# Quarter sums of the adjacency made by adding DRAM transfers, and layer 2 of the last two pairs run apart, in a four-layer graph network

## The chip, the cores and the metric

The kernel runs on one core of one Trainium2 chip. The metric is the device time of one execution in microseconds (us), given as the median of several runs. One further execution was profiled; the traces and the page below are of that one.

## What is computed

Inputs are `x` (8 batches, 2048 nodes, 64 channels, float32) and one 2048 x 2048 matrix `adj`. Four layers follow each other, each with a residual and a layer norm:

```
# layer 0: y0 = x, y1 = A x, y2 = 2 A y1 - x; node-wise weights from a 16-wide embedding
out = einsum('bnki,nkio->bno', x_g, w) + b
# layer 1: masked attention, att = softmax(where(adj > .5, leaky(s1_i + s2_j), -9e15))
h_prime = einsum('bij,bjc->bic', att, h);  elu
# layer 2: agg = einsum('ij,bjh->bih', adj + I, x W^T + b) / deg
# layer 3, three times: effects = A v;  v = relu([v, effects] W1^T + b1) W2^T + b2
x = layernorm(x + layer(x))        # after each layer
```

Almost all of the multiplying is the product of `A` (or `A + I`) with a 2048-row matrix: twice per batch in layer 0, once in layer 2, three times in layer 3, and the attention product of layer 1.

## The kernel before, in words

**Tiles.** Two batches of 64 channels make a pair; there are four pairs, and a pair's activations fill a 128-column matrix of 16 row tiles in SBUF (`SX[p]`, and the shared buffers `SA`, `SB`, `SH`). The transposed matrix stays in DRAM. It is read in tiles of 128 partitions x 2 x 512 float32, 512 KB each, 32 to a sweep (4 column chunks `c` by 8 row blocks `q`). A tile is loaded by the SP queue into a ring of six buffers (`a_ring`, `fetch`, `refill`), in the order of the list `order_of_a`. One sweep for one pair is 64 matmuls of 128 x 512 (line 1093), each in two float32 passes. Results of a chunk are accumulated in one of two PSUM banks (`acc_ring`).

**Order.** All engines' instruction orders are written at build time by a planner (class `Plan`): each thread (a Python generator) names the engine that it wants next and what it waits for, and the planner runs the one that can begin first, by ready time and then by rank. What comes out is one fixed order for each engine. The sweeps have the lowest rank (1000) and fill TensorE.

**Stages.** TensorE makes the layer-0 products first (`first_product`, `second_product`, and line 601 for the node-wise weights), then layer 2 and the three steps of layer 3 for pair 0 and then for pair 1, and meanwhile the attention products (line 836) of all pairs, for which VectorE works nearly without a pause: it finds row maxima over mask rows `mr` (line 731, `scores`), and adds and subtracts rows for the weights (lines 809 and 822, `weights`). Mask rows (`mr`, 512 KB) and mask columns (`mk`, 256 KB), and the broadcast rows `s2b`, `s1b` and `mb` (1 MB each) are loaded by the GpSimd (POOL) queue, which also stores.

**The last two pairs** are handled jointly, because one product of a 2048 x 2048 matrix with a 2048 x 256 matrix can be made in seven quarter products instead of eight. The quarters of `A` are a11, a12, a21, a22 (first index: output half, second: contracted half); those of the right side are B11, B21 (first pair `p`) and B12, B22 (second pair `o`).

- `joint_layer2` (line 1188) does layer 2 of both pairs at once: each tile of `A` is loaded once and used for both pairs (line 1212), four PSUM banks being open. The four tiles at the same place in the four quarters come one after the other, and thread `sums` (line 1159) makes from them on VectorE, in tiles of 128 x 1024 (line 1172), s1 = a21 + a22, s2 = s1 - a11, s3 = a11 - a21 and s4 = a12 - s2. Each is stored to DRAM by the POOL queue (line 1174). Where the tile in SBUF holds `A + I`, `pure` (line 1149) loads the plain tile once more.
- `joint_layer3` (line 1247) does the three steps with the seven products a11 B11, a12 B21, s2 T1, s3 T2, a22 T3, s1 T0, s4 B22 (line 1299). The T are differences of the B (`sums_of_u`). Parts of the result are put together on VectorE (`combine`), and the v-term of the layer is added by a seed matmul (line 1284, and line 1347 for one quarter).

After a product's chunk come short chains over several engines. After layer 2: copy out of PSUM (`z_evict`), product with W (line 981), residual and norm on VectorE and ScalarE, transposes (line 1015), product for `u` (line 1028). After a step of layer 3: relu (`h_evict`), then line 1028, or line 1048 and the final norm and store (`last_chunk`, `store`).

Priority of the scores: `layer1` starts `scores(p)` with rank `10 + p`, and its loads of `s2b` wait in the planner until all mask rows are stored (`"rows"`).

Of the kernel before, what the change touches and what calls it, by code (L numbers as in the profile page):

```python
# [17 lines left out]
P = 128  # L18
# [6 lines left out]
B = 8  # L25
# [118 lines left out]
def resnorm_d4_kernel(  # L144
# [182 lines left out]
    for e in range(2):  # L327
# [20 lines left out]
        for m in ("s1", "s2", "s3", "s4")  # L348
# [84 lines left out]
    def row_tile(t, an, k, done):  # L433
        yield "ACT", [done]
        dg = tiny([P, 1], "dg", 2)
        nc.scalar.activation(an, an, AF.Copy, accum_out=dg)
        done = plan.run("ACT", act(N) + 0.2, done)
        yield "DVE", [done, mr_ring]
        nc.vector.tensor_scalar_add(dg, dg, 1.0)
        nc.vector.reciprocal(rdeg[:, t : t + 1], dg)  # L440
        mk, km = mr_ring.take([P, N], "mr", BF16)
        nc.vector.tensor_scalar(mk, an, THRESHOLD, NEG_INF, ALU.is_le, ALU.mult)
        done = plan.run("DVE", 1.13 + 0.26, done)
        bc_ring.give(k, done)
        nc.gpsimd.dma_start(by_row[t], mk)
        done = plan.dma("DMA", 512, done)
        mr_ring.give(km, done)
        at["by_row", t] = done
        if all(("by_row", i) in at for i in range(NT)):
            at["rows"] = done  # L450
# [208 lines left out]
    def layer1(p):  # L659
# [38 lines left out]
        plan.start(10 + p, scores(p, sv, xc, s_rows, done))  # L698

    def scores(p, sv, xc, s_rows, done):  # L700
        s2b = []
        for e in range(2):
            yield "DMA", [bc_ring, done, "rows"]
# [228 lines left out]
    JOINT = (NPAIR - 2, NPAIR - 1)  # L932
# [9 lines left out]
    def z_evict(p, c, pa, give, done):  # L942
# [4 lines left out]
        give(done)  # L947
# [180 lines left out]

    RQ = AQ // 2

    def quarters(k, r):

        return [(k, r), (k, r + RQ), (k + 2, r), (k + 2, r + RQ)]

    def order_of_joint():
        for k in range(2):
            for r in range(RQ):
                order_of_a.extend((c, q, True) for c, q in quarters(k, r))
        for s in range(3):
            for m in ("a11", "a12", "s2", "s3", "a22", "s1", "s4"):  # L1140
                i, j = {"a11": (0, 0), "a12": (0, 1), "a22": (1, 1)}.get(m, (0, 0))
                for k in range(2):
                    for r in range(RQ):
                        if m[0] == "a":
                            order_of_a.append((k + 2 * i, r + RQ * j, False))
# [3 lines left out]
    def pure(k, r):  # L1149

        yield "SP", [("group", k, r), *([xg_ring] if len(xg_ring.freed) > 1 else [NEVER])]
        got = []
        for c, q in (quarters(k, r)[i] for i in (0, 3)):
            t, kt = xg_ring.take([P, 2, CW], "pure")
            nc.sync.dma_start(t, tile_of_adj(c, q))
            got.append((t, kt, plan.dma("SP", 512, xg_ring.t)))
        return got

    def sums(k, r, taken):

        tiles4 = [(t, kt, got) for t, kt, got, _ in taken]
        own = {}
        if r // 2 == k:
            own = dict(zip((0, 3), (yield from pure(k, r))))
        a11, a12, a21, a22 = ((own.get(i) or tiles4[i])[0] for i in range(4))
        ready = [(own.get(i) or tiles4[i])[2] for i in range(4)]

        def out_of(m, a, b, op, *after):
            yield "DVE", [bc_ring, *after]
            t, kt = bc_ring.take([P, 2, HALF], m)  # L1170
            t = t.rearrange("p a b -> p (a b)")[:, 0 : 2 * CW].rearrange("p (t n) -> p t n", n=CW)
            nc.vector.tensor_tensor(t, a, b, op)
            done = plan.run("DVE", dve(2 * CW), *after)
            nc.gpsimd.dma_start(sum_tiles[m][k, r], t)  # L1174
            bc_ring.give(kt, plan.dma("DMA", 512, done))
            return t, done

        s3, d3 = yield from out_of("s3", a11, a21, ALU.subtract, ready[0], ready[2])
        s1, d1 = yield from out_of("s1", a21, a22, ALU.add, ready[2], ready[3])
        s2, d2 = yield from out_of("s2", s1, a11, ALU.subtract, d1)  # L1180
        s4, d4 = yield from out_of("s4", a12, s2, ALU.subtract, d2)
        for (_, kt, _, free), d in zip(taken, (d2, d4, d1, d1)):
            a_ring.give(kt, max(free, d))
        for _, kt, _ in own.values():
            xg_ring.give(kt, d2)
        refill()

    def joint_layer2():
        p, o = JOINT
        at["group", 0, 0] = 0.0  # L1190
        for k in range(2):
            pas = {}
            for r in range(RQ):
                taken = []
                for i, (c, q) in enumerate(quarters(k, r)):
                    n = next(used)
                    if r == 0 and i in (0, 2):
                        if i == 0:
                            yield "PE", [po_ring, ("x2", p), ("x2", o)]
                            t2, kp = po_ring.take([P, 2, CW], "po")  # L1200
                            pas[c] = [(t2[:, e, :], kp) for e in range(2)]
                        else:
                            pas[c] = []
                            for e in range(2):
                                yield "PE", [acc_ring]
                                pas[c].append(acc_ring.take([P, CW], "acc"))
                    for e, pair in enumerate(JOINT):
                        yield "PE", [("a", n)]
                        t, kt = a_tiles[n]
                        for b in range(2):  # L1210
                            m = 2 * q + b
                            nc.tensor.matmul(
                                pas[c][e][0],
                                lhsT=SX[pair][:, m, :],
                                rhs=t[:, b, :],
                                start=(r == 0 and i in (0, 2) and b == 0),
                                stop=(r == RQ - 1 and i in (1, 3) and b == 1),
                            )
                        done = plan.run("PE", mm(CW, 2), ("a", n))
                        if r == RQ - 1 and i in (1, 3):  # L1220
                            if i == 3:
                                give = lambda t, kk=pas[c][e][1]: acc_ring.give(kk, t)
                            else:
                                give = give_half(pas[c][e][1])
                            plan.start(1, z_evict(pair, c, pas[c][e][0], give, done))
                    del a_tiles[n]
                    taken.append((t, kt, at["a", n], done))
                    if i == 0:
                        nxt = (k, r + 1) if r + 1 < RQ else (k + 1, 0)
                        at[("group", *nxt)] = plan.free["PE"]  # L1230
                    spent[0] += 1
                plan.start(5, sums(k, r, taken))
                refill()

    halves_left = {}

    def give_half(kp):
        def give(t):
            left, last = halves_left.pop(kp, (2, 0.0))
            if left == 1:  # L1240
                po_ring.give(kp, max(t, last))
            else:
                halves_left[kp] = (1, max(t, last))

        return give

    def joint_layer3():
        p, o = JOINT
        U, _ = e_ring.take([P, 2, HALF], "u23")
        T12, _ = e_ring.take([P, 2, HALF], "t12")  # L1250
        T34, _ = e_ring.take([P, 2, HALF], "t34")
        T = [
            t[:, i, :].rearrange("p (t n) -> p t n", n=P) for t in (T12, T34) for i in range(2)
        ]
        for s in range(3):
            up, uo = u_of(p, s), u_of(o, s)
            B11, B21, B12, B22 = up[:, 0:8], up[:, 8:16], uo[:, 0:8], uo[:, 8:16]
            plan.start(0, sums_of_u(s, T, B11, B21, B12, B22))
            u = lambda pair, half: lambda k: ("u", pair, s, 2 * half + k)
            t = lambda i: lambda k: ("t", s, i, k)  # L1260
            seed = gv if s else w31v
            held = {}

            for m, B, need, evict, seeded in (
                ("m1", B11, u(p, 0), None, None),
                ("m2", B21, u(p, 1), None, (p, 0)),
                ("m6", T[1], t(1), "u2", None),
                ("m7", T[2], t(2), "u3", None),
                ("m4", T[3], t(3), "c21", (p, 1)),
                ("m5", T[0], t(0), "c22", None),  # L1270
                ("m3", B22, u(o, 1), "c12", (o, 0)),
            ):
                for k in range(2):
                    if m == "m2":
                        pa, ka = held[k]
                        yield "PE", [("m1", s, k)]
                    else:
                        yield "PE", [acc_ring, need(0)]
                        pa, ka = acc_ring.take([P, CW], "acc")
                    go_on = m == "m2"  # L1280
# [197 lines left out]
```

## Time and profile before

| | us |
|---|---|
| median of 3 runs | 2132.62 (2131.99 to 2137.06) |
| the profiled execution | 2133.99 |
| its span in the trace | 2132.2 |
| TensorE busy / idle in the span | 2067.3 / 64.9 |
| VectorE busy | 1496.4 |
| joint layer 2 begins / joint layer 3 begins / last large matmul ends | 1652 / 1782 / 2121 |
| granted TensorE clock, mean | 0.994 |

How to read the profile: engines are PE (TensorE matmul), PEld (its weight loads), DVE (VectorE), ACT (ScalarE), POOL (GpSimd) and SP (SyncE). `L1093` is line 1093 of the kernel. In a table of windows each row gives the stretch, its length, then for each engine the busy time and (x...) its instructions, then the granted clock, the share of the 16 DMA engines' time that is busy, and GB/s. In a timeline, each row gives start, duration, engine, line, operation, output and inputs, and in brackets how long the engine was idle before it and what ended that. A float32 matmul is recorded as two passes, so 64 matmuls show as x128.

### The profile page before, as it was taken

To read this page: it belongs to the slowest core of one execution; us is meant where nothing else is said; L and a number is where in the kernel's file an instruction comes from. 1 tells how busy PE (TensorE), PEld (TensorE's weight loads), DVE (VectorE), ACT (ScalarE), POOL (GpSimd) and SP (SyncE) were. 2 spreads that over 40 slices of the span, in tenths; PEclk is the share of its full clock that TensorE was granted. 3 is DMA by queue.
4 is the path that set the end of the run, shared out by engine and by line. 5 is a ranking of instruction groups with operands and counts; after the bars stand their busy time and mean duration, and the time that the engine had idled before them with its cause. 6 is when DMAs were issued, how large, how long until landed. Compare 5 with 4: busy or idle time off the path is not lost. (4 is left out here: it accounts for less than half of the span.)

```text
span 2132.2 us, 19037 instructions
## 1 busy us (share of the span) xinstructions
PE 2067.3 (97%) x6325; PEld 914.9 (43%) x6325; DVE 1496.4 (70%) x1908; ACT 974.9 (46%) x1794; POOL 213.0 (10%) x374
## 2 busy tenths in 40 slices
PE   8999999999999999999798999989999999999998
PEld 3444444433433443433343453443444444444444
DVE  2226647998799999789998979999796455120214
ACT  0025424567776566777624857336575012000002
POOL 2310000100110100000010101011010110000000
PEclk9999999999999999999899999999999999999999
DMA  9799835634443465554388778897776777878785
GB/s 303 267 333 345 306 105 209 218 122 136 138 137 131 159 238 169 170 178 150 124 309 299 254 267 285 279 339 239 264 236 234 290 255 273 280 254 281 251 288 188
DMA packets 208740, 495.85 MB, mean 233 GB/s; under 512 B 20274, under 2 KB 28594, under 8 KB 204530
## 3 DMA queue, kind: packets, MB, share of 16 engines
q1 hardware_dynamic: 165058, 347.62, 48.0%
q0 software_dynamic: 39360, 144.92, 19.7%
q10 hardware_dynamic: 4224, 2.10, 0.4%
q8 instruction: 50, 0.82, 0.2%
q14 instruction: 48, 0.39, 0.1%
HBM read 446.14 MB, written 46.33 MB: 231 GB/s over the span
## 5 line engine op out<-in xcount | busy, mean ns | idle before, releaser
L1093 PE MATMUL acc<-a,SX 128*128 128x512 f32 x1024 | 465.8, 598 | 9.6 <-DMA SX<-in_x 6.6
L1093 PE MATMUL acc<-a,SA 128*128 128x512 f32 x768 | 348.6, 596 | 13.1 <-DMA a<-in_adj_t 12.4
L817 ACT ACTIVATE e<-e,sv 128x1024 f32<-128x1024 f32 x256 | 280.1, 1154 | 114.4 <-DVE e L809 110.6
L731 DVE CUSTOM_DVE_ANT_0 junk<-s2b,mr 128x2048 bf16<-128x2048 f32 x128 | 292.7, 2287 | 5.2 <-DMA mr<-by_row 3.9
L624 ACT ACTIVATE terms<-yp,emb_sb 128x128 f32<-128x128 f32 x896 | 243.5, 400 | 113.6 <-PE yp L601 113.3
L1093 PEld LDWEIGHTS acc<-a,SX 128*128 128x128 f32 x1024 | 190.3, 191 | 242.2 <-issue 229.6
L822 DVE TENSOR_TENSOR e<-e,mb 128x2048 f32<-128x2048 f32 x128 | 290.0, 2286 | 6.0 <-ACT e L817 5.4
L809 DVE TENSOR_TENSOR e<-s1b,mk 128x2048 f32<-128x2048 f32 x128 | 289.1, 2286 | 6.5 <-PE po L836 4.0
L825 ACT ACTIVATE e<-e 128x2048 f32<-128x2048 f32 x128 | 245.0, 1928 | 67.5 <-DVE e L822 67.2
L601 PE MATMUL yp<-SH,xgT 128*128 128x512 f32 x512 | 246.9, 607 | 3.3 <-ACT sv L358 3.3
L836 PE MATMUL po<-e,SX 128*64 128x512 f32 x1024 | 235.4, 602 | 3.1 <-ACT e L825 3.1
L1093 PEld LDWEIGHTS acc<-a,SA 128*128 128x128 f32 x768 | 140.9, 190 | 186.0 <-issue 166.0
L1299 PE MATMUL acc<-a,t 128*128 128x512 f32 x384 | 168.7, 592 | 0.0
L636 DVE TENSOR_TENSOR terms<-terms 128x512 f32<-128x512 f32 (+1 forms) x176 | 130.0, 738 | 42.2 <-ACT terms L624 38.2
L601 PEld LDWEIGHTS yp<-SH,xgT 128*128 128x128 f32 x512 | 90.9, 189 | 145.7 <-issue 137.6
L836 PEld LDWEIGHTS po<-e,SX 128*64 128x64 f32 x1024 | 68.1, 137 | 155.8 <-issue 133.7
L601 PE MATMUL yp<-SH,y2T 64*128 64x512 f32 x512 | 128.3, 617 | 0.0
L804 POOL DMA_DIRECT2D mk<-by_col x128 | 69.0, 540 | 546.7 <-DVE e L809 452.1
L1093 PE MATMUL acc<-a,SB 128*128 128x512 f32 x256 | 118.3, 595 | 0.0
L1299 PEld LDWEIGHTS acc<-a,t 128*128 128x128 f32 x384 | 72.0, 190 | 86.1 <-issue 86.1
L601 PEld LDWEIGHTS yp<-SH,y2T 64*128 64x128 f32 x512 | 43.6, 186 | 79.9 <-issue 76.4
L1093 PEld LDWEIGHTS acc<-a,SB 128*128 128x128 f32 x256 | 47.2, 190 | 57.3 <-issue 57.3
(225 smaller groups left out, 1677.7 us busy)
## 6 DMA issues: line engine op xcount, KB each, us to landing
a<-in_adj_t SPq DMA_DIRECT2D x496, 512.0 KB, 5.5
a<-s SPq DMA_DIRECT2D x96, 512.0 KB, 4.5
mr<-by_row POOLq DMA_DIRECT2D x64, 512.0 KB, 5.9
mk<-by_col POOLq DMA_DIRECT2D x128, 256.0 KB, 5.0
an<-in_adj SPq DMA_DIRECT2D x16, 1024.0 KB, 10.7
s<-s POOLq DMA_DIRECT2D x32, 512.0 KB, 5.0
a<-a_plus_i SPq DMA_DIRECT2D x24, 512.0 KB, 5.0
by_col<-mk POOLq DMA_DIRECT2D x32, 256.0 KB, 5.8
```

The lines of the kernel that those rows point to most:

```text
L601: nc.tensor.matmul(yp[:, e, :], lhsT=y2T[rows, cs] if k2 else xg[:, e, cs], rhs=(wk2 if k2 else w01)[rows, hs], start=(k2 == h), stop=(k2 ...
L624: nc.scalar.activation(batches(terms[0][:, dd, :]), term, AF.Copy, scale=weight)
L636: nc.vector.tensor_tensor(a, a, b, ALU.add)
L731: nc.vector.tensor_tensor_reduce(out=junk, in0=s2b[e][0], in1=masks[t][0], scale=1.0, scalar=LOWEST, op0=ALU.add, op1=ALU.max, accum_out=m ...
L804: nc.gpsimd.dma_start(mk, by_col[jt // 2][:, jt % 2, h * HALF : (h + 1) * HALF])
L809: nc.vector.tensor_tensor(e, s1b[0], mk.unsqueeze(1).to_broadcast([P, 2, HALF]), ALU.add)
L817: nc.scalar.activation(e[:, i, :], e[:, i, :], AF.Prelu, bias=sv[:, 2 + i, jt : jt + 1], alpha=ALPHA)
L822: nc.vector.tensor_tensor(e, e, mb[0], ALU.add)
L825: nc.scalar.activation(e, e, AF.Exp)
L836: nc.tensor.matmul(po[i * C : (i + 1) * C, f, :], lhsT=SX[p][:, t, i * C : (i + 1) * C], rhs=e[:, i, f * CW : (f + 1) * CW], start=(t == 0 ...
L1093: nc.tensor.matmul(pa, lhsT=source[:, m, :], rhs=t[:, i, :], start=(m == 0 and not seed), stop=(m == NT - 1),)
L1299: nc.tensor.matmul(pa, lhsT=B[:, 2 * r + b, :], rhs=at_[:, b, :], start=(r == 0 and b == 0 and not go_on), stop=(r == RQ - 1 and b == 1), ...
```

## The change

The four sums of quarters are now sa = a12 + a22, sb = a11 + a12, sc = sa + a11 and sd = sc + a21. They are made in DRAM, by the POOL queue alone: one transfer copies a 512 KB tile from DRAM to DRAM, and a later one adds another tile to it (`accum_op`). There are 8 tiles of each sum, so 32 copies and 32 adding transfers; the planner may start them from its time 320 us on, one each 14 us. `sums`, `pure` and `joint_layer2` are gone. Layer 2 of pair 2 and of pair 3 are two ordinary sweeps, one after the other; each of their tiles is loaded for one pair. The joint layer 3 uses other seven products, in another order and with the roles of the two pairs exchanged (`JOINT`). `scores` no longer waits for `"rows"`, and has rank 1.2 for pair 0 and `9.5 + p` for the others.

```
-        for m in ("s1", "s2", "s3", "s4")
+        for m in ("sa", "sb", "sc", "sd")
...
-        plan.start(10 + p, scores(p, sv, xc, s_rows, done))
+        plan.start(1.2 if p == 0 else 9.5 + p, scores(p, sv, xc, s_rows, done))
...
-            yield "DMA", [bc_ring, done, "rows"]
+            yield "DMA", [bc_ring, done]
...
-    JOINT = (NPAIR - 2, NPAIR - 1)
+    JOINT = (NPAIR - 1, NPAIR - 2)
...
+    def sums_of_a():
+        n = itertools.count()
+        for m, a, b in (
+            ("sa", "a12", "a22"),
+            ("sb", "a11", "a12"),
+            ("sc", "sa", "a11"),
+            ("sd", "sc", "a21"),
+        ):
+            for x in (a, b):
+                for k, r in sum_tiles[m]:
+                    if x in QUARTER:
+                        part = tile_of_adj(k + QUARTER[x][0], r + QUARTER[x][1])
+                    else:
+                        part = sum_tiles[x][k, r]
+                    before = [("sum", m, k, r)] if x == b else []
+                    if x not in QUARTER:
+                        before.append(("sum", x, k, r, True))
+                    yield "DMA", [320.0 + 14.0 * next(n), *before]
+                    nc.gpsimd.dma_start(
+                        sum_tiles[m][k, r], part, **({"accum_op": ALU.add} if x == b else {})
+                    )
+                    done = plan.dma("DMA", 900 if x == b else 512) + 1.0
...
-            for m in ("a11", "a12", "s2", "s3", "a22", "s1", "s4"):
+            for m in ("sb", "a11", "sc", "sd", "a21", "a22", "sa"):
...
-    def pure(k, r):
-    def sums(k, r, taken):
-    def joint_layer2():
...
+            for k in range(2):
+                pa, ka = banks[k] = acc_ring.take([P, CW], "acc")
+                done = yield from quarter(pa, B22, u(o, 1), True)
+                plan.start(1, keep(s, k, pa, done))
...
+                seeded(o, k, pa, False)
+                done = yield from quarter(pa, T3, t(3), False)
...
+                done = yield from quarter(pa, T1, t(1), True)
...
+                done = yield from quarter(pa, B11, u(p, 0), True)
+                plan.start(1, z_and_v(s, k, pa, ka, done))
...
+                seeded(o, 2 + k, pa, True)
+                done = yield from quarter(pa, T6, t(6), False)
...
+                done = yield from quarter(pa, T7, t(7), True)
...
+                seeded(p, k, pa, False)
+                done = yield from quarter(pa, T4, t(4), False)
...
-            for s in range(4):
+        for p in range(NPAIR):
+            for s in range(4 if p < NPAIR - 2 else 1):
                 order_of_a.extend((c, q, s == 0) for c, q in sweep_of_a)
...
+        yield from sweep(layer2_product(NPAIR - 2))
 
         yield "PE", [("x2", NPAIR - 1)]
...
-        yield from joint_layer2()
+        yield from sweep(layer2_product(NPAIR - 1))
         yield from joint_layer3()
...
+    plan.start(1, sums_of_a())
```

In the new `joint_layer3`, T3 = B12 - B22, T1 = B11 + B22, T6 = B11 + B12, T7 = B22 - B21 and T4 = B21 - B11; `quarter` is the inner loop that line 1299 had before, four tiles of two matmuls for each product and chunk.

## The prediction

> **What bounds the kernel now.** I read the page first: busy times, then the slices.
>
> ```profile
> PE 2067.3 (97%) x6325; PEld 914.9 (43%) x6325; DVE 1496.4 (70%) x1908; ACT 974.9 (46%) x1794; POOL 213.0 (10%) x374
> PE   8999999999999999999798999989999999999998
> DVE  2226647998799999789998979999796455120214
> DMA  9799835634443465554388778897776777878785
> ```
>
> TensorE is idle for 2132.2 - 2067.3 = 64.9 us of the span; VectorE is nearly full from slice 8 to slice 29, and has room in the joint stage at the end. A built order of both programs shows 3299 matmul instructions before and 3299 after, and lets me count the others: TensorE's work is the same, so the change can only move the 64.9 us. Fifty-us windows place them: 13 in the first 300 us, 3 from 300 to 1000, 15.1 from 1000 to 1050, 7.2 from 1100 to 1150, 1.0 to 1200, 6.7 from 1400 to 1450, 8.8 from 1650 to 1800, 10.1 in the tail.
>
> ```profile
> 320.00:1050.00 730.00, 711.90 (x2198) 291.99 (x2198) 666.91 (x763) 494.78 (x1101) 74.34 (x136) 0.99 0.50 163
> 1050.00:1100.00 50.00, 50.00 (x185) 24.94 (x182) 47.96 (x47) 21.87 (x25) 3.32 (x7) 1.00 0.72 238
> 1100.00:1150.00 50.00, 42.80 (x122) 18.98 (x120) 41.98 (x47) 14.13 (x17) 7.67 (x14) 1.00 0.98 359
> 1150.00:1200.00 50.00, 48.97 (x156) 19.70 (x158) 49.97 (x32) 33.83 (x27) 4.83 (x9) 1.00 0.67 227
> 1650.00:1800.00 150.00, 141.25 (x454) 71.74 (x453) 81.53 (x146) 26.39 (x65) 17.82 (x33) 1.00 0.75 266
> 1800.00:2100.00 300.00, 300.00 (x818) 142.70 (x817) 60.91 (x101) 22.89 (x42) 3.03 (x4) 1.00 0.81 274
> ```
>
> The second last column is the DMA share. Two rows matter: in 1100 to 1150 the DMA engines are full and TensorE loses 7 us; in 1650 to 1800, the joint layer 2, it loses 9 us with DMA to spare. TensorE's timeline there shows what the 9 us are:
>
> ```profile
> 1723.24 0.66 PE L1015 MATMUL ps_vT<-ident,SX 128*128 128x128 f32 x4 [1.59 <-DVE SX L510]
> ...
> 1727.28 0.63 PE L1015 MATMUL ps_vT<-ident,SX 128*128 128x128 f32 x4 [1.54 <-DVE SX L510]
> 1728.58 1.16 PE L1028 MATMUL ps_u<-w31e,h_o 128*128 128x128 f32 x8 [0.67 <-ACT h_o L358]
> ...
> 1792.56 0.63 PE L1015 MATMUL ps_vT<-ident,SX 128*128 128x128 f32 x4 [1.33 <-DVE SX L510]
> ```
>
> Four chains of layer-2 tails start at once, and TensorE waits for their norms. And the stall at 1120:
>
> ```profile
> 1124.71 1.98 PE L1093 MATMUL acc<-a,SA 128*128 128x512 f32 x4 [2.30 <-DMA a<-in_adj_t]
> 1128.37 3.70 PE L1093 MATMUL acc<-a,SA 128*128 128x512 f32 x8 [1.68 <-DMA a<-in_adj_t]
> ```
>
> There a tile of A is spent each 1.72 us (four passes), 524 KB / 1.72 = 305 GB/s, and mask and row loads of the POOL queue come on top: in 1095 to 1135 a tile takes 9.1 us to land, against 5.2 us in 1800 to 2100.
>
> **What the Trainium skill says.** (1) "DMA: Bandwidth & Descriptors", SWDGE vs HWDGE vs iDMA: adding during a transfer is only to be had on GpSimd's queue. The built order agrees: all 64 transfers stand there, among the loads of `mr` and `mk`. (2) Same page, Queues, rings and completion order: each DMA engine goes round-robin between the queues that have work. So SP's tiles don't wait for a whole backlog of POOL's, but share with it; the 9.1 us above agree. (3) "Collectives: The Full Stack", The bandwidth ceiling: an addition costs a transfer its second source read, and halves the rate (1.93 measured there). No trace here shows one. (4) "Perfetto Trace Analysis", Identifying the Most-Contended Engine: matmul busy time is no measure of distance from the peak. Here it is close all the same: 16 passes take 6.87 us (1652.14 to 1659.01), 0.429 us each, with no more between them.
>
> **The change part by part.**
>
> *Joint layer 2 becomes two sweeps.* Removed: the stalls of 1650 to 1800. By the timeline they are 0.66 + 0.68 + 1.59 + 1.54 + 0.67 + 0.67 + 0.31 + 0.35 + 1.33 + 0.88 = 8.7 us. In the built order each tail's steps (981, 1015, 1028) now stand 2 to 5 tile steps of 1.72 us apart, one chain at a time; and the joint layer 3 begins with sb B22 of pair 2, whose layer 2 ended a sweep (55 us) ago. What pair 3's last chunk must deliver is wanted two products, 2 x 14.6 = 29 us, later, and its chain took about 13 us before (1784.06 to 1797.11). Gain 8.7 us; I leave 0.7 for waits that the order doesn't cover: 8.
>
> The price: 64 tiles in 110 us instead of 32 tiles each used twice, 305 GB/s. The joint layer 3 draws 274 GB/s at a share of 0.81 without one us of idle, and the 8 `pure` loads and 32 stores fall away (40 x 0.5 MB). I take 0; were it not covered, a stall as at 1120 would cost some us.
>
> *VectorE's sums go.* 32 x 1.22 us = 39 us, from rows like this one:
>
> ```profile
> L1172 DVE TENSOR_TENSOR s<-a,s 128x1024 f32<-128x1024 f32 x8 | 9.8, 1224 | 1.5 <-DMA s<-s 1.3
> ```
>
> VectorE was busy 81.5 of 150 us there: worth nothing beyond the stalls already counted. The first sweep of layer 2 no longer waits for pair 3's attention, which gives VectorE 55 us more; it wasn't late (TensorE idle 0.7 us from 1600 to 1700), so 0.
>
> *The new seven products.* Seven by 16 matmuls and 8 seeds a step, as before. Of the waits, `m5`, `x`, `z` and `c21` each have a chunk (6.9 us) in front of them, and need one PSUM read: 0.69 us (VectorE) or 0.59 (ScalarE) by the rows of lines 1367 and 1339, and up to 1.2 us until it starts. The seed of `z_and_v` stands in TensorE's stream three or so matmul pairs behind its chunk. From step to step, c11 comes last: c, relu, u, T1 are about 0.7 + 0.7 + 1.0 + 0.7 + 0.7 us and their handovers, 7 us, with 29 us cover. I take 0; should one passage a step stand open by 2 us, 6 us in all. The tail (10.1 us) keeps its steps.
>
> *The 64 transfers.* At 1110 to 1130 the engines move 392 to 396 GB/s at share 1.0, so a copy of 524 KB costs 1.33 us of all 16. An addition: from below a copy's price, 1.33; from (3) twice that, 2.7; from above four times, 5.3, if reading the target doesn't overlap. I take 2.7. In all 32 x 1.33 + 32 x 2.7 = 129 us in 880 us, share +0.15 on 0.55: on the average there is room. They do harm where there is none. By their neighbours in POOL's order, against the times of these neighbours before, between 1087 and 1140 stand the copy into sd_13 and the additions to sd_00, sd_01 (right before `s1b` and `mb`) and sd_02: 1.33 + 3 x 2.7 = 9.4 us more where the share is already 0.98. Up to all of it falls on TensorE's tiles, at a half share two thirds: 6 to 9, I take 8. In 1150 to 1200 four more (10.7 of 50 us) lift 0.67 to 0.88: 1 us. Before 1050 the full stretches (400 to 420, 740 to 750) have two products to a tile, 3.4 us, and TensorE didn't wait in them: 0. POOL's issuing, 64 x 0.7 us, is hidden (10% busy). Behind an addition on POOL's queue wait `mr` and `mk`, with three buffers each: an `mk` is due 3 x 4.57 = 13.7 us after its buffer is free and lands in 4.2, so 2.7 us more is covered.
>
> *Rank of the scores.* In the built order pair 0's maxima move ahead of pair 1's term sums for some 60 us of VectorE, and by 560 us both orders run level again; TensorE's are equal, row by row, for the next 180 rows, to about 1130. VectorE waits for layer 0 again at 890 to 920 (12 us idle), so a lead won early is lost there. I take 0, bounds -3 and +4.
>
> Sum: -8 + 8 + 1 = +1 on the execution's 2134.0, 2135. That execution was 1.4 us over the median shown: 2133.6, I say 2134.
>
> **The rivals.**
>
> A. *The additions hardly collide* (price near a copy's, or served in gaps): 1.33 x 4 = 5.3 us, of which the slack in 1080 to 1090 (0.81) and the round-robin leave 1. -8.7 + 1 on 2132.6: 2125. For it: the mean share of 0.55. Against: 9 of 10 us from 1090 on are full.
>
> B. *Slower: the additions hold the POOL queue in front of `mb` and `mk` of pair 2's first half.* At 5.3 us each, 1.3 + 3 x 5.3 = 17 us at 1087 to 1140, and 4 x 5.3 + 0.67 x 50 = 55 us of work in the 50 us to 1200: 17 + 5 - 8.7 = +13, 2146. VectorE's e-chain starts later, and TensorE's line 836 waits in order for it. It decides from about 4.5 us an addition on. For it: nothing shows an addition; every second one stands right before a load that VectorE needs. Against: skill (3). If additions take 10 us or more, all mask loads from 430 us on are late by more than their cover: 2170.
>
> C. *The gain isn't there*: TensorE's waits at 1650 to 1800 come back as waits for tiles, now that each is used once. Then 2134 + 5 = 2139. For it: nothing to spare at 1120. Against: row 1800 to 2100.
>
> **How the numbers follow.** What a measurement can tell from no change is about 0.3%, 6.4 us: 2126 to 2139. Likeliest case 0.43 (2128 to 2139); A 0.26; B 0.21, and 0.05 with the 2170; C 0.05. Faster 0.27, within 0.43, slower 0.30. The range leaves out half of A's better part and the worst of B: 2120 to 2154.
>
> **What would show it.** Idle before line 1015 and 1028 in the two layer-2 sweeps under 1 us: step one right. An adding transfer's landing time against a copy's gives the price. TensorE's idle in the stretch of pair 2's `s1b` and `mb`: 15 us for me, 8 for A, over 20 for B. Wrong altogether if TensorE's idle grows before 1000, or if its busy time differs by more than 3 us.

## The result, and the profile after

| | before | after |
|---|---|---|
| median, us | 2134.4 (2132.0 to 2140.1, 9 runs) | 2142.5 (2139.3 to 2147.1, 9 runs) |
| span of the profiled execution | 2132.2 | 2138.2 |
| TensorE busy / idle | 2067.3 / 64.9 | 2078.5 / 59.7 |
| VectorE / GpSimd busy | 1496.4 / 213.0 | 1459.9 / 252.7 |
| granted clock, mean | 0.994 | 0.988 |

The ratio is 1.0037 [1.0022, 1.0051]: slower by 8 us. TensorE waits 5.2 us less than before and is busy 11.2 us longer with the same matmuls. The busy times and VectorE's row of slices of the page after:

```profile
PE 2078.5 (97%) x6325; PEld 920.3 (43%) x6325; DVE 1459.9 (68%) x1876; ACT 978.6 (46%) x1794; POOL 252.7 (12%) x406
...
DVE  2226647998799999879998979999797323121214
```

The windows after, in the stretches that were shown of before (the third last column is the granted clock):

```profile
320.00:1050.00 730.00, 711.78 (x2182) 291.14 (x2178) 661.06 (x746) 490.06 (x1093) 119.85 (x189) 0.99 0.66 202
1050.00:1100.00 50.00, 47.15 (x173) 22.74 (x174) 46.88 (x51) 24.95 (x30) 4.75 (x9) 0.91 0.58 188
1100.00:1150.00 50.00, 43.64 (x121) 20.27 (x120) 47.07 (x59) 10.17 (x19) 12.79 (x19) 0.97 1.04 366
1150.00:1200.00 50.00, 46.91 (x137) 18.50 (x137) 43.96 (x31) 28.47 (x23) 7.79 (x12) 0.93 0.94 293
1650.00:1800.00 150.00, 150.00 (x478) 76.77 (x477) 49.35 (x124) 29.20 (x70) 1.53 (x2) 1.00 0.81 269
1800.00:2100.00 300.00, 300.00 (x827) 143.42 (x827) 59.77 (x100) 24.27 (x46) 2.25 (x3) 1.00 0.81 269
```

Three things are to be seen. In 1650 to 1800 TensorE doesn't wait at all: the stalls of layer 2 are gone, and the tiles for the two separate sweeps arrive in time. In 1150 to 1200 the DMA share has gone from 0.67 to 0.94. And the clock is down in three of the first four rows, where before it was 0.99 or 1.00 (in 1050 to 1100 in part because the low clock at the end of layer 0, which ended at 1049 before, now lasts until 1059). TensorE's timeline names the waits:

```profile
475.12 1.94 PE L834 MATMUL po<-e,SX 128*64 128x512 f32 x8 [1.35 <-ACT e L823]
...
478.72 0.63 PE L669 MATMUL ps_xT<-ident,SX 128*128 128x128 f32 x4 [1.66 <-DVE SX L508]
...
689.33 0.66 PE L562 MATMUL ps_xg<-ident,SX 128*128 128x128 f32 x4 [3.50 <-ACT terms L622]
...
1137.02 3.56 PE L1091 MATMUL acc<-a,SA 128*128 128x512 f32 x4 [2.04 <-DMA a<-in_adj_t]
...
1149.30 1.98 PE L1091 MATMUL acc<-a,SX 128*128 128x512 f32 x4 [1.66 <-DMA a<-in_adj_t]
...
1153.21 2.69 PE L1091 MATMUL acc<-a,SX 128*128 128x512 f32 x4 [1.93 <-DMA a<-in_adj_t]
```

Where the 6 us between the two spans lie: the first number is TensorE's idle time in us, the second the time lost to half clock. The clock's record has short spells in which only half of the full clock was granted; half of the busy time inside them counts as lost.

| stretch | before | after | more |
|---|---|---|---|
| 0 to 300 | 13.0 + 1.7 | 12.2 + 3.2 | +0.7 |
| 300 to 1000 | 3.0 + 0 | 8.0 + 1.7 | +6.7 |
| 1000 to 1100 | 15.1 + 3.1 | 13.1 + 6.4 | +1.3 |
| 1100 to 1250 | 8.2 + 0 | 9.4 + 4.5 | +5.7 |
| 1250 to 1650 | 6.6 + 0 | 5.7 + 2.7 | +1.8 |
| 1650 to 1800 | 8.8 + 0 | 0 + 0 | -8.8 |
| 1800 to the end | 10.1 + 0 | 11.3 + 0 | +1.2 |

They sum to 8.6; 2.6 us of the other sign stay unassigned. (Both runs end in a spell of half clock, but it begins after the last matmul and costs TensorE nothing.) The half clock in short spells was no part of my working. In the clock's record each spell but the last of a run lasts a multiple of 3.41 us, and all spells of a run begin on one grid of 3.41 us. Four windows of that grid, after:

```profile
1133.90:1137.30 3.40, 1.36 (x4) 0.47 (x3) 3.37 (x3) 0.00 (x0) 1.43 (x2) 1.00 0.96 332
1137.30:1140.70 3.40, 3.40 (x5) 1.36 (x5) 2.91 (x4) 0.09 (x1) 0.38 (x2) 0.50 1.01 417
1140.70:1144.10 3.40, 3.40 (x14) 1.58 (x13) 1.55 (x2) 0.60 (x1) 0.40 (x1) 1.00 1.04 399
1147.50:1150.90 3.40, 1.75 (x5) 0.68 (x4) 3.40 (x3) 3.37 (x4) 1.32 (x3) 1.00 1.10 268
```

TensorE is busy for 1.36 us of the first, so idle for 2.04, and the next runs at 0.50: a tile step takes 3.56 us in place of 1.98. The last has 1.65 us of idle, and the window after it runs at full clock.

### The profile page after: what moved, and what is told of

It reads as the page before. It is cut to its first block, busy times and chain, and to the rows that moved or that the text cites. A ratio compares the mean times of both kernels' runs of the same rounds, so it can differ in the third digit from the quotient of the medians.

```text
span 2138.2 us, 19049 instructions
## 1 busy us (share of the span) xinstructions
PE 2078.5 (97%) x6325; PEld 920.3 (43%) x6325; DVE 1459.9 (68%) x1876; ACT 978.6 (46%) x1794; POOL 252.7 (12%) x406
## 3 DMA queue, kind: packets, MB, share of 16 engines
q0 software_dynamic: 46272, 161.70, 24.5%
## 4 chain that ended last, share of the span: by engine, by line
PE 51%; issue 26%; DVE 16%; ACT 3%; DMA 3%; POOL 0%; SPq 0%; POOLq 0%; DVEq 0%; ACTq 0%
PE acc L1091 29%; PE yp L599 11%; PE po L834 7%; DVE junk L729 4%; DVE e L807 3%; DVE e L820 3%; DVE terms L634 2%; DMA a<-in_adj_t 2%; ACT e L815 1%; ACT terms L622 1%; PE ps_u L1026 1%; DMA an<-in_adj 1%; PE acc L1080 1%; PE pf L868 1%; ACT e L823 0%
## 5 line engine op out<-in xcount | busy, mean ns | idle before, releaser
L1091 PE MATMUL acc<-a,SX 128*128 128x512 f32 x1280 | 585.3, 602 | 15.8 <-DMA SX<-in_x 6.6
L1091 PEld LDWEIGHTS acc<-a,SX 128*128 128x128 f32 x1280 | 238.4, 192 | 305.3 <-issue 281.2
L820 DVE TENSOR_TENSOR e<-e,mb 128x2048 f32<-128x2048 f32 x128 | 290.3, 2285 | 10.9 <-ACT e L815 10.6
L1204 PE MATMUL acc<-a,t 128*128 128x512 f32 x192 | 85.4, 592 | 0.0
L489 ACT ACTIVATE ln_sq<-SX 128x512 f32<-128x512 f32 x48 | 30.7, 640 | 101.9 <-DVE SX L992 44.0
## 6 DMA issues: line engine op xcount, KB each, us to landing
an<-in_adj SPq DMA_DIRECT2D x16, 1024.0 KB, 10.6
```

The lines of the kernel that those rows point to most:

```text
L820: nc.vector.tensor_tensor(e, e, mb[0], ALU.add)
L1091: nc.tensor.matmul(pa, lhsT=source[:, m, :], rhs=t[:, i, :], start=(m == 0 and not seed), stop=(m == NT - 1),)
L1204: nc.tensor.matmul(pa, lhsT=B[:, 2 * r + b, :], rhs=at_[:, b, :], start=(start and r == 0 and b == 0), stop=(r == RQ - 1 and b == 1), skip ...
```

## The experiments

All ratios are to the kernel before, run on the same chip, with 95% intervals. My first theory after the result was that the rank of the scores makes the lag that stands from 550 us on, and the transfers the loss at 1100 to 1250; the rival, that the transfers make both.

**1. The rank undone.**

```
-        plan.start(1.2 if p == 0 else 9.5 + p, scores(p, sv, xc, s_rows, done))
+        plan.start(10 + p, scores(p, sv, xc, s_rows, done))
```

and `"rows"` as in the kernel before.

> The changed kernel with one part undone: the scores have rank 10 + p again and wait for all mask rows, as before. Theory 1 (order): the other rank delays VectorE by the 8.25 us by which every step from 550 to 1050 us stands later after the change; undone, the time falls by about 8 us, to a ratio to the kernel before of 1.000, and the lag of the last layer-0 step at 1053 us goes to under 2 us. Theory 2 (transfers): the 64 transfers make that lag, by late mask and tile loads; the rank is worth less than 2 us, the ratio stays at 1.0037 and the lag at 8 us.

Ratio 1.0003 [0.9995, 1.0012]: 7 us of the 8 are gone. TensorE's idle in 300 to 1000 is 3.0 us again, and the waits at 475, 478 and 689 are not there. The last wait of layer 0 still ends 3.2 us later than before (1.5 us of it is a spell of half clock near 250 us, before the transfers begin), not under 2. It is shown before, in the changed kernel and in this run:

```profile
1044.58 0.48 PE L1015 MATMUL ps_vT<-ident,v 128*128 128x128 f32 x1 [7.42 <-DVE v L1007]
...
1052.85 0.48 PE L1013 MATMUL ps_vT<-ident,v 128*128 128x128 f32 x1 [7.50 <-DVE v L1005]
...
1047.73 0.47 PE L1015 MATMUL ps_vT<-ident,v 128*128 128x128 f32 x1 [7.41 <-DVE v L1007]
```

Of the two edits only one acts. With the rank alone undone the planner writes the same order on every engine as here, and so it does when only pair 0 gets its old rank; with `"rows"` alone put back the order is that of the changed kernel. So the rank of 1.2 for pair 0 is all that acts.

**2. The rank alone, on the kernel before.** The same two edits the other way round.

> The kernel before with that one part done alone: rank 1.2 for pair 0's scores and 9.5 + p for the others, no wait for all mask rows. Theory 1 (order): 8 us slower than before, ratio 1.004, with the steps from 550 to 1050 us some 8 us later. Theory 2 (transfers): within 2 us of before, ratio 0.999 to 1.001.

Ratio 1.0022 [1.0013, 1.0032]: +4.7 us, not 8. The sign is as expected, but the planner lays the rest out differently, and the loss comes elsewhere: 16 us at the end of layer 0 are won, and more is lost where pair 3's attention ends in front of the joint layer 2:

```profile
1630.87 5.35 PE L834 MATMUL po<-e,SX 128*64 128x512 f32 x16 [2.45 <-ACT e L823]
...
1641.87 5.15 PE L834 MATMUL po<-e,SX 128*64 128x512 f32 x16 [5.64 <-ACT e L823]
```

So what a rank costs is a property of the order that the planner makes of it, not of one step.

**3. No transfers.**

```
-                    nc.gpsimd.dma_start(
-                        sum_tiles[m][k, r], part, **({"accum_op": ALU.add} if x == b else {})
-                    )
...
-            src = sum_tiles[c][q]
+            src = tile_of_adj(q[0], q[1])
```

> The changed kernel with the 64 transfers that make the sums left out; where a sum's tile would be loaded, a plain tile of the matrix is loaded, so the joint layer 3 multiplies by other numbers. All orders are those of the changed kernel. Theory 1 (order): only the loss at 1100 to 1250 us goes, 6 us, ratio 1.001. Theory 2 (transfers): both that and the 8 us before 1050 go, what is left is the gain of 8.75 us in layer 2, ratio 0.996.

Ratio 1.0000 [0.9992, 1.0009]: the transfers cost 8 us; between both expectations (1.001 and 0.996), nearer the first. The orders are those of the changed kernel, so this is the price of the transfers themselves. The layer-0 row shown under run 1 stands at 1052.28, in the changed kernel at 1052.85: half a microsecond of the lag was the transfers'. The rival falls. Two windows of this kernel, in which TensorE's idle is 5.1 us and no spell of half clock falls:

```profile
1100.00:1150.00 50.00, 45.97 (x131) 21.61 (x130) 49.42 (x58) 13.07 (x21) 8.72 (x16) 1.00 0.99 371
1150.00:1200.00 50.00, 48.98 (x160) 19.89 (x159) 47.58 (x33) 33.42 (x27) 5.59 (x10) 1.00 0.78 268
```

The landing times in 1105 to 1170 show how the transfers get at TensorE. First the changed kernel, then this one (tensors, queue, count, KB, median us to landing):

```profile
a<-in_adj_t SPq DMA_DIRECT2D x23, 512.0 KB, 10.0
sd<-in_adj_t POOLq DMA_DIRECT2D x5, 512.0 KB, 13.3
mk<-by_col POOLq DMA_DIRECT2D x7, 256.0 KB, 12.7
```

```profile
a<-in_adj_t SPq DMA_DIRECT2D x28, 512.0 KB, 7.4
mk<-by_col POOLq DMA_DIRECT2D x7, 256.0 KB, 5.8
```

With the five additions among them the loads shown take longer to land. Six buffers at 1.72 us a tile cover 8.6 to 10.3 us (an estimate, five or six tile steps); 7.4 is inside that, 10.0 at its edge.

**4. Copies in place of additions.** `**({"accum_op": ...})` is dropped from the call.

> The changed kernel with its 32 adding transfers made plain copies of the same tiles, so that the sums are not sums. By the trace an addition costs some 3.2 us of all 16 DMA engines where I took 2.7, a copy 1.3; the GpSimd queue's share should fall by 32 x 1.9 = 61 us, 2.9 points of the span. Theory 1 (order): about half of the 6 us at 1100 to 1250 goes, ratio 1.002. Theory 2 (transfers): half of 14 us, ratio 1.000.

Ratio 1.0015 [1.0007, 1.0022], as theory 1 expected (1.002). The GpSimd queue's share, changed kernel and this one:

```profile
q0 software_dynamic: 46272, 161.70, 24.5%
```

```profile
q0 software_dynamic: 42176, 161.70, 22.2%
```

24.5% of 2138.2 less 22.2% of 2141.8 is 48 us: an addition costs 1.5 us of all 16 engines more than a copy (I had expected 61 us and 1.9). Without the transfers the share is 17.7% of 2130.7, so a copy costs (475 - 377) / 64 = 1.5 us and an addition 3.0.

**5. Layer 2 alone.** Edits 1 and 3 together.

> Layer 2 alone: the changed kernel with the rank of the scores undone and the 64 transfers left out (plain tiles of the matrix are loaded in the sums' place, so the joint layer 3 multiplies by other numbers). If the three parts add up, what is left is the gain of two separate sweeps of layer 2, 8.75 us of stalls: 8 us faster than before, ratio 0.996. If the gain is lost somewhere even without the transfers, the ratio stays at 0.999 to 1.000, and the trace shows idle of TensorE after 1100 us that the kernel before doesn't have.

Ratio 0.9970 [0.9958, 0.9982], 6.4 us faster. The four runs add up: from 1.0037, the rank takes 0.0034 (run 1) or, without transfers, 0.0030 (3 to 5); the transfers take 0.0037 (3) or, without the rank, 0.0033 (1 to 5); layer 2 gives 0.0030. Of layer 2's 8.8 us some come back: one wait of 3.25 us for ScalarE at 1161, and about 2 us at the end.

**6 and 7. The same sums at other times.** On run 1's kernel:

```
-                    yield "DMA", [320.0 + 14.0 * next(n), *before]
+                    yield "DMA", [320.0 + 10.5 * next(n), *before]
```

> All sums made, rank of the scores undone, and the transfers started each 10.5 us from 320 us on, so that the last one starts at about 990 us and none falls into 1050 to 1250. If transfers cost time only where tiles of the matrix are short (my theory now): nearly the time of the kernel without them, ratio 0.996 to 0.998, and TensorE's idle in 1100 to 1250 as in the kernel before. If they cost time wherever they lie, by mask loads that wait behind them: ratio 1.000 or more, and VectorE waits for masks before 1000 us.

```
+                    i = next(n)
+                    start = 320.0 + 12.0 * i if i < 56 else 1450.0 + 14.0 * (i - 56)
+                    yield "DMA", [start, *before]
```

> All sums made, rank undone, 56 of the transfers started each 12 us from 320 us on, and the last eight additions each 14 us from 1450 us on, where the DMA engines are busy at 0.68 to 0.80. If the collision at 1100 to 1250 is the whole loss: ratio 0.996 to 0.998. If an addition next to a sweep that takes a tile each 1.7 us costs TensorE time in any place: some 8 x 1 us, ratio 1.001, idle for tiles at 1450 to 1600.

Ratios 0.9963 [0.9951, 0.9975] and 0.9939 [0.9923, 0.9955], the second better than I expected. Both keep 1100 to 1250 free of additions, and TensorE's idle there is 4.2 and 5.0 us, with no half clock; run 6 loses some of it at the end of layer 0, where it waits for `e` (5.7 us at 1006). In run 7 TensorE is full beside the late additions, though the share is 0.93:

```profile
1100.00:1150.00 50.00, 45.04 (x129) 19.65 (x128) 48.99 (x53) 18.18 (x22) 8.54 (x16) 1.00 1.00 366
1150.00:1200.00 50.00, 50.00 (x159) 20.52 (x158) 49.31 (x28) 35.19 (x27) 4.32 (x8) 1.00 0.69 232
...
1450.00:1550.00 100.00, 100.00 (x335) 42.61 (x334) 84.78 (x66) 65.29 (x57) 17.43 (x24) 1.00 0.93 290
```

These two ratios are no clean price of a transfer's time, though. Run 5 has no transfers at all, and run 7 is 6.6 us faster than that. The planner makes a new order for new start times: runs 3 and 4 have the order of the changed kernel and run 5 that of run 1, but runs 6 and 7 have orders of their own. TensorE's idle in 1100 to 1250 is 10.6 us in run 5 and 5.0 in run 7, and neither has additions there. So what run 7 gains over run 5 can only come of the order, and how much of its gain over run 1 is the transfers' is not shown.

**8. Waits on purpose.** In the changed kernel, ahead of each product of the joint steps, a small matmul, a round over VectorE of 512 (first step) or 2048 columns (second), and a matmul that reads what it wrote:

```
+                nc.tensor.matmul(pt[:, 0:P], lhsT=ident, rhs=ident, start=True, stop=True)
...
+                size = 2048 if s else 512
+                nc.vector.tensor_copy(w[:, 0:P], pt[:, 0:P])
+                nc.vector.tensor_tensor(w[:, P:size], ones[:, P:size], ones[:, P:size], ALU.add)
+                nc.vector.tensor_copy(w[:, 0:P], w[:, size - P : size])
...
+                nc.tensor.matmul(pt[:, 0:P], lhsT=ident, rhs=w[:, 0:P], start=True, stop=True)
```

> The changed kernel with TensorE made to wait on purpose: in the first of the three joint steps seven waits for a short round over VectorE (about 1.4 us each), in the second step seven longer ones (about 3 us each), none in the third. Theory (clock): a window of 3.41 us in which TensorE is idle over about 2 us brings a spell of half clock some 10 us after; so the first step grows by its waits alone, 7 x 1.4 = 10 us with no low clock, and the second by 7 x 3 = 21 us and by 1.7 us for each low window, four to seven of them, 28 to 33 us in all. Rival (the low clock has nothing to do with idle): both grow by their waits alone, and low windows stand where they stood in the changed kernel.

Span 2177.1. Waits of 1.5 us, as at 1812 in the first fence, brought no low clock at all in the first step. In the second step other matmuls filled most of five of the seven waits (0.3 to 1.4 us were left); the two that stood open (2.7 and 3.2 us) each brought a spell, together three low windows, fewer than the four to seven expected, and there are no others from 1650 to the tail. The first of them by windows follows in the second fence.

```profile
1812.57 0.49 PE L1220 MATMUL ps_stall<-wait,ident 128*128 128x128 f32 x2 [1.60 <-DVE wait L1217]
...
1938.45 0.49 PE L1220 MATMUL ps_stall<-wait,ident 128*128 128x128 f32 x2 [2.71 <-DVE wait L1217]
```

```profile
1935.90:1939.30 3.40, 0.85 (x4) 0.61 (x5) 2.46 (x3) 0.25 (x1) 0.00 (x0) 0.99 0.87 308
1939.30:1942.70 3.40, 3.40 (x6) 1.34 (x5) 0.00 (x0) 0.00 (x0) 0.00 (x0) 0.50 0.07 28
1942.70:1946.10 3.40, 3.40 (x10) 1.49 (x9) 0.00 (x0) 0.00 (x0) 0.00 (x0) 1.00 0.44 147
```

The rival (clock and idle have nothing to do with each other) falls, on two planted waits of one run. One thing in my expectation was wrong: "some 10 us after" came from a record whose zero lies 10.5 us ahead of the span's; it is the very next window.

**9 and 10. Both losses apart, and both edits at other times.** Run 9 puts run 7's start times into the changed kernel, rank and all. Run 10 is run 1 with `320.0 + 14.0 * i if i < 48 else 1450.0 + 10.0 * (i - 48)`.

> The changed kernel with one edit: 56 of the transfers each 12 us from 320 us on, the last eight additions from 1450 us on. If rank and transfers are two separate losses: the 8 us of the transfers go, those of the rank stay, ratio 1.000, and the waits for ScalarE and VectorE of 8 us in 300 to 1000 us stand as in the changed kernel. If the rank hurts only together with the transfers' places: ratio 0.994, as with both edits.

> Both edits again, at other times: rank undone, 48 transfers each 14 us from 320 us on as in the changed kernel, the last sixteen (copies and additions of sd) each 10 us from 1450 us on. If it is only the stretch of 1050 to 1250 us that must be kept free: ratio 0.993 to 0.997, with TensorE's idle at 1100 to 1250 no more than 8 us. If the ratio of 0.994 was the luck of one order or of the windows of the clock: 0.998 or more.

Run 9: 0.9993 [0.9982, 1.0005], the number expected of two separate losses, but not by their path. Its order is again another one: the waits in 300 to 1000 are 5.8 us (8.0 in the changed kernel, 3.0 before), the last wait of layer 0 ends at 1036.03, before even the 1044.58 of the kernel before, and against run 7 the rank costs 11.5 us, which in the traces lie after 1100. That the two losses are separate is shown by runs 1, 3 and 5, not by this run. Run 10: 0.9938 [0.9925, 0.9951], median 2122.7 beside 2136.1; its order differs from run 7's in a few places, so run 7 was not the luck of one exact order. Runs 7 and 10 beat both kernels, with all sums made.

## Why the prediction was right in its time, and where its steps failed

I forecast 2134 in a range of 2120 to 2154; it came to 2142.5. The time was inside, but my likeliest case (no change that can be told) was not the one that came. My sum was +1 us and +8 was measured; that the time lay inside is owed to the width of the range and not to the sum, in which a term of 7 us stood at 0.

- **Joint layer 2, -8.** Right: 8.8 us of waits in 1650 to 1800 became 0, there is no wait ahead of lines 1013 and 1026 in the two sweeps, and rival C falls (no wait for a tile either). In the time it was worth 6.4 us (run 5), in the order that the planner made there; between runs 5 and 7 another order alone was worth as much, so the 8.8 us of waits are surer than the 6.4.
- **VectorE's sums and the new seven products, 0.** Right as far as the trace shows: TensorE doesn't wait from 1650 until the tail, which is 1.2 us longer.
- **An addition's price, 2.7.** 3.0 measured (run 4), twice a copy's 1.5. What I took from the Trainium skill, "Collectives: The Full Stack", The bandwidth ceiling (1.93), agrees with the ratio of 2.0.
- **The transfers, +8 and +1.** The sum was right, 7 to 8 us (runs 1, 3 and 5), and before 1050 they cost next to nothing, as said. The place, 1087 to 1200, fits the changed kernel only: against run 5, run 1 loses 3.5 us in 1100 to 1250 and 4.9 in 1250 to 1650 (idle and half clock). My sign for them was not right: I named 15 us of idle for my case and 8 for A. The idle at 1100 to 1250 was 9.4, only 1.2 more than before; 4.5 us of the loss came as half clock, which I hadn't in the sum. Rival B's mechanism was half there: loads of `mk` land after 12.7 us in place of 5.8, and VectorE is busy 2.4 us less in 1100 to 1150 and 3.6 less in 1150 to 1200 than in run 3, but TensorE's waits there name the tiles of `A`, not `po`.
- **Rank of the scores, 0 with bounds -3 and +4.** This is the step that failed: 6.4 to 7.3 us after the change (runs 1, 3, 5), 4.7 on the kernel before (run 2). I argued that the orders run level again by 560 us, and that a lead won early is lost while VectorE waits at 890. I took no account of a delay. In the changed kernel VectorE comes out of the reordered stretch late, after a wait of 6.5 us up to 545 for ScalarE's `terms`, and this isn't made up (the first row is before, the other two after):

```profile
907.73 2.41 DVE L636 TENSOR_TENSOR terms<-terms 128x1024 f32<-128x1024 f32 x3 [6.10 <-ACT terms L624]
...
544.84 2.41 DVE L634 TENSOR_TENSOR terms<-terms 128x1024 f32<-128x1024 f32 x3 [6.50 <-ACT terms L622]
...
915.97 2.41 DVE L634 TENSOR_TENSOR terms<-terms 128x1024 f32<-128x1024 f32 x3 [6.10 <-ACT terms L622]
```

The very wait that I counted on is as long after as before, 6.10 us, only 8.2 us later: what VectorE waits for there had become late too. TensorE's `ps_vT` of 1044.58 is at 1052.85, 8.3 us later (1.5 of them the half clock near 250). Orders that are level at a row say nothing of the time at which that row is reached. That the rank makes the loss is shown by runs 1 and 5; that it does so by this one wait is read from the trace and not shown. Runs 2 and 9 have a like wait of 6.1 us up to 530 and 528, and run 9 then ends layer 0 early.

- **"TensorE's work is the same, so the change can only move the 64.9 us."** It failed too. Busy time rose by 11.2 us. Cleared of half clock (4.8 us before, 18.6 after) it is 2062.5 and 2059.9, within the 3 us that I named; the matmuls are the same, their speed is not. Both of my signs of being wrong altogether came: this one, and TensorE's idle before 1000, which grew by 4 us.

The Trainium skill speaks of the half clock in "TensorE: Matmul & The Clock Gate", Part 1: a clock of half rate follows an idle window of about 3.4 us, on a free-running grid. The grid and the 3.41 us agree with the records here. That a whole window has to be idle doesn't: some 2 us of 3.41 were enough.

## What to carry to other kernels

Price a wait of a nearly full TensorE by where it falls: here idle of under 1.85 us within one window of 3.41 us cost itself, over 2.05 us cost itself and, in a full window after it, 1.7 us more. Ask of background transfers beside what they run, not only how many they are: the additions at 1110 to 1207 stood beside waits for tiles, those of run 7 at 1446 to 1547 beside none. Where a planner writes the order, a new start time is also a new order, so price a load between kernels of one order. And undo the small edits beside the large one first: the largest term that I had put at zero was a rank.

## What was not expected of the hardware

- Over all twelve traces, from 10 to 2100 us: of TensorE's windows at full clock with 1.0 to 1.85 us of idle on the 3.41 us grid, none of 136 was followed by a window at half clock; of those with more than 2.05 us, all of 51 were; between them five of ten. Idle is not the only cause: every trace has one spell at about 79 us, after a window without any idle, and nothing here explains it.
- Once at half clock, less idle sufficed to keep the next window low too: 0.6 us or more did in 39 of 39 low windows after that first spell, under 0.5 us in none.
- The grid isn't tied to the program: with the same instructions up to about 290 us, the wait near 248 us (2.94 us before, 2.87 after) brought a spell in the changed kernel and none before, where an edge of the grid at 250.0 cut it in two. That alone is 1.5 us between two executions.
